# Silu made from Tanh, and products taken out of PSUM in their own step, in the first stage of a two-layer kernel

## The chip, the cores and the metric

The kernel runs on one core of a Trainium2 chip. The metric is the device time of one execution in microseconds; it is the median over several executions. The core has five queues that work in order and side by side: TensorE (PE, with its weight loads shown as PEld), VectorE (DVE), ScalarE (ACT), GpSimd (POOL) and SyncE (SP), which issues most DMAs.

## The reference

All tensors are fp32. The input x is 8 batches of 512 tokens of 256 channels. The first layer adds a state-space branch and an FP4-quantized gated network to x; the second layer adds two attention branches. Only the first layer is touched:

```
xn   = layernorm(x)
# branch 1: selective scan, 512 inner channels, 16 states
xin, z = split(xn @ W_in.T)
u    = silu(conv4(xin) + conv_b)              # causal, per channel
dt, B, C = split(u @ W_xproj.T)
delta = softplus(dt @ W_dt.T + b_dt)
h_t  = exp(delta_t * A) * h_{t-1} + (delta_t * u_t) * B_t
y    = (sum_n h * C + D * u) * silu(z)
out1 = y @ W_out.T
# branch 2: weights, xn and h are rounded to blocks of 16 FP4 values with a scale
h    = silu(fp4(xn) @ fp4(w_gate).T) * (fp4(xn) @ fp4(w_up).T)
out2 = fp4(h) @ fp4(w_down).T
x    = x + out1 + out2
```

## The kernel before

The work of the first layer, called the first stage, is written as one program order for all engines: in this stage every engine executes its instructions exactly in the order in which the Python program issues them, and every instruction has the helper's line, L53, in the profile. Its instructions are therefore told apart by the names of their tiles.

**The scan loop.** The backbone is a loop over g, 256 steps: 8 batches, 4 channel chunks of 128, and 8 pairs of the 16 states. Step g issues, in this order: the load of C for step g + 2 (tile cb, on SP's queue); `scan`, two VectorE scans of 128x512 (hh from da and bu); `decay` for step g + 2, two ScalarE Exp (da); in odd steps `inputs`, 16 small groups of PE matmuls that spread delta*u times B over the states into the one PSUM buffer bu, which serves the next two steps and so can't begin before the odd step's scans have ended; `sum_states`, PE transposes that add the states of earlier steps into y; one `step()` of the strands; and `times_c`, GpSimd's product of hh with C.

**The strands.** All other work is cut into generators, called strands, which advance by one stage in each `step()`, by rank. `z` and `finish` come first (the gate z of a chunk, and y's way out through a transpose to the product with z), then `output` (W_out), then the delta strands and `diagonals`, then `head` (layer norm, transposes xt, projections, convolution, u, and the product ps_xp), then `ffn` (branch 2), then the FP4 rounding of the weights. `head` of batch b + 1 starts 16 steps before batch b does; while the next but one step of the loop has not its delta, du and B ready (`able`), `step()` is called again without a scan, so that the loop stands still.

A strand's stages are given as functions to `skewed`, which runs one stage of each unit per step. A stage that makes a product on PE allocates one of three PSUM banks (MM = 3, tag mm); the tuple at a stage says how many banks it frees and takes, and a strand is passed over in a step if it would take more than are free. In the kernel before, a product and its way out of PSUM are two stages, so a bank is held from one step into the next. The ones that matter:

- `head`: `project` (PE, ps_in), `tap0` (ScalarE, cv = first tap and bias), `taps12` and `tap3` (VectorE, three multiply-adds that read ps_in and cv), `silu` (ScalarE, u): five steps, two between the starts of two chunks. Then ps_xp, and in the next step its copies xd and xb.
- The delta strand: `rank` (PE, ps_dt), `parts` (ScalarE: Relu, Abs, Exp, Copy), `rests` (VectorE, tile e), `logs` (ScalarE, Ln), `deltas` (GpSimd, from the second batch on), `turned` (PE, ps_du), `put_du` (ScalarE): seven steps; a chunk every three steps.
- `ffn`, for each of 4 token tiles: the gate's product (ps_gu from w_g); a step later ScalarE's Silu into h and the up product (ps_gu from w_u); a step later VectorE's h * ps_gu; this for two halves of 352 columns, then the FP4 rounding (q_m on ScalarE, q_l and q_v on VectorE, q_v and h on GpSimd), the transposes `to_inner` (ps_i, taken out into ht) and w_down (ps_d).
- `z`: the product ps_z; a step later ScalarE's Silu into z.
- `finish`: ScalarE's copy of y (into the tile delta), PE's transpose ps_y, VectorE's u * D + ps_y, GpSimd's product with z.

ScalarE holds one function table at a time; where the next function isn't in it, the program has an ACT_TABLE_LOAD ahead of that instruction. The functions of this stage are Exp, Ln, Sqrt, Silu, and Identity, Copy, Abs and Relu, ahead of which no load stands.

The second layer's stage follows, with other loops and no Silu; it is not part of the change.

Of the kernel before, what the change touches and what calls it, by code (L numbers as in the profile page):

```python
# [9 lines left out]
FP = mybir.dt.float32  # L10
BF = mybir.dt.bfloat16
AF = mybir.ActivationFunctionType
ALU = mybir.AluOpType
# [4 lines left out]
P = 128  # L18
# [40 lines left out]
def tile_kernel(ctx: ExitStack, tc: tile.TileContext, a: dict, out: bass.AP):  # L59
# [57 lines left out]
    with ExitStack() as s0:  # L117
# [36 lines left out]
        def constants():  # L154
            act.activation(a_neg, a_neg, AF.Exp)
            dve.tensor_scalar(a_neg, a_neg, -1.0, None, ALU.mult)
            dve.tensor_reduce(four, ident.rearrange("p (r n) -> p n r", n=QL), AX.X, ALU.add)
            n = FI - (NI - 1) * P
            for t in (w_d, *hts):
                pool.memset(t[n:, NI - 1, :], 0.0)  # L160

        w_g = w0.tile([P, KC, FI], FP, name="w_g")
        w_u = w0.tile([P, KC, FI], FP, name="w_u")
        def skewed(units, stages, every):


            made = {}
            stages = [s if isinstance(s, tuple) else (s, 0, 0) for s in stages]
            for step in range((len(units) - 1) * every + len(stages)):
                todo = [(i, stages[step - i * every]) for i in range(len(units)) if 0 <= step - i * every < len(stages)]  # L170
                peak = held = 0
                for _, (_, frees, takes) in todo:
                    held += takes - frees
                    peak = max(peak, held)
                yield peak, held
                for i, (f, _, _) in todo:
                    made[i] = f(units[i], made.get(i))
# [86 lines left out]
        def to_inner(dst, then=()):  # L264


            def turn(src, c0, c1):
                ps = pmm.tile([P, L], FP, tag="mm", name="ps_i")
                for c in range(c0, c1):
                    n = min(P, FI - c * P)  # L270
                    pe.transpose(ps[:n, (c - c0) * P : (c - c0 + 1) * P], src[:, c * P : c * P + n], ident)
                return src, ps

            def both(unit, st):
                src, ps = st
                out = dst(unit)
                act.copy(out[:, :4, :], ps.rearrange("p (c n) -> p c n", n=P))
                return out, turn(src, 4, NI)[1]

            def last(unit, st):  # L280
                out, ps = st
                n = FI - (NI - 1) * P
                act.copy(out[:, 4, :], ps[:, :P])
                act.copy(out[:n, 5, :], ps[:n, P : 2 * P])
                return out

            return [(lambda _, src: turn(src, 0, 4), 0, 1), (both, 1, 1), (last, 1, 0)]

        def fp4_weights():
# [14 lines left out]
            def turn(unit, raw):  # L304
                ps = pmm.tile([P, L], FP, tag="mm", name="ps_w")
                for k in range(KC):
                    for i in range(2):
# [4 lines left out]
                        )  # L312
                return ps

            def put(unit, ps):
                name, at = unit
                dst = w_g if name == "w_gate" else w_u
                act.copy(
                    dst[:, :, at * FB : (at + 2) * FB],
                    ps[:, : 4 * FB].rearrange("p (k n) -> p k n", k=KC),  # L320
                )

            down = to_inner(lambda unit: w_d[:, :, unit[1] * P : (unit[1] + 1) * P])
            units = [(name, j) for j in range(0, FI // FB, 2) for name in ("w_gate", "w_up")]
            stages = [fetch, idle, *fp4_stages(FB, 2 * D), (turn, 0, 1), (put, 1, 0)]
            yield from skewed(units, stages, 2)
# [31 lines left out]
        def head(b):  # L358
# [29 lines left out]
            def turn(k, _):  # L388
                ps = pmm.tile([P, L], FP, tag="mm", name="ps_tr")
                for t in range(NT):  # L390
                    pe.transpose(ps[:, t * P : (t + 1) * P], xn[:, t, k * P : (k + 1) * P], ident)
                return ps

            def put(k, ps):
                act.copy(xt[:, k, :], ps)

            yield from skewed(range(KC), [(turn, 0, 1), (put, 1, 0)], 1)

# [4 lines left out]
            def project(c, _):  # L403
                ps = pmm.tile([P, L], FP, tag="mm", name="ps_in")
                for k in range(KC):
                    pe.matmul(
                        ps, w_in[:, k, c * P : (c + 1) * P], xt[:, k, :], start=(k == 0), stop=(k == KC - 1)
                    )
                return ps

# [4 lines left out]

            def tap0(c, ps):
                cv = rot.tile([P, L], FP, tag="cv", bufs=2, name="cv")
                act.activation(
                    cv, ps, AF.Identity, scale=conv_w[:, c, 3:4], bias=conv_b[:, c : c + 1]
                )  # L420
                return ps, cv

            def taps12(c, st):
                tap(st[1], st[0], c, 1)
                tap(st[1], st[0], c, 2)
                return st

            def tap3(c, st):
                ps, cv = st
                tap(cv, ps, c, 3)  # L430
                return cv

            def silu(c, cv):
                u_.setdefault(b, []).append(w1.tile([P, L], FP, tag="u", bufs=2 * NC + 2, name="u"))
                act.activation(u_[b][c], cv, AF.Silu)

            while b - 3 in u_:
                yield 0, 0
            stages = [(project, 0, 1), tap0, taps12, (tap3, 1, 0), silu]
            yield from skewed(range(NC - 2), stages, 2)  # L440
# [4 lines left out]
            while b > 1 and (b - 2, NC - 1) not in ready:  # L445
                yield 0, 0
            yield 1, 1
            ps = pmm.tile([P, L], FP, tag="mm", name="ps_xp")
            for c in range(NC):
                pe.matmul(ps, w_xp[:, c, :], u[c], start=(c == 0), stop=(c == NC - 1))  # L450
            yield 0, -1
            xd = w1.tile([P, L], FP, tag="xd", bufs=1, name="xd")
            act.copy(xd, ps)
            xb = rot.tile([P, L], FP, tag="e", bufs=3, name="xb")[:NS]
            act.copy(xb.rearrange("n (t r j) -> n r t j", t=NT, j=QL), ps[:NS].rearrange("n (r t j) -> n r t j", t=NT, j=QL))
            c_d = dram.tile([NS, L], FP, tag="c_d", name="c_d")
            sp.dma_start(c_d, xd[RC : RC + NS, :])
            diags = diags_[b] = []

            def diagonals():  # L460
# [10 lines left out]
                for i in range(NS // 4):  # L471
                    yield (0, -1) if i == NS // 4 - 1 else (0, 0)
                    bd = rot.tile(shape, FP, tag="bd", bufs=2 * (NS // 4) - 1, name="bd")
# [8 lines left out]
            def rank(c):  # L482
                ps = pmm.tile([P, L], FP, tag="mm", name="ps_dt")
                pe.matmul(ps, w_dt[:, c * P : (c + 1) * P], xd, start=True, stop=True)
                return ps

            def parts(c, ps):
# [5 lines left out]
                act.activation(w, ps, AF.Copy, bias=1.0)  # L493
                return ps

# [18 lines left out]
            def turned(c, _):  # L514
                ps = pmm.tile([P, L], FP, tag="mm", name="ps_du")
                for t in range(NT):
                    pe.transpose(ps[:, t * P : (t + 1) * P], du[b, c][:, t * P : (t + 1) * P], ident)
                return ps

            def put_du(c, ps):  # L520
                act.copy(du[b, c], ps)
                ready.add((b, c))

            by = pool if b else dve
            begin(diagonals(), 2)
            stages = [
                (lambda c, _: rank(c), 0, 1), parts, (rests, 1, 0), logs, deltas, (turned, 0, 1), (put_du, 1, 0),
            ]
# [8 lines left out]
        def ffn(b):  # L537
# [14 lines left out]
            def turn_x(k, _):  # L552
                ps = pmm.tile([P, L], FP, tag="mm", name="ps_tr")
                for t in range(NT):
                    pe.transpose(ps[:, t * P : (t + 1) * P], xn[:, t, k * P : (k + 1) * P], ident)
                return ps

            def put_x(k, ps):
                act.copy(xqt[:, k, :], ps)

            yield from skewed(range(KC), [(turn_x, 0, 1), (put_x, 1, 0)], 1)
            quantized.add(b)
# [11 lines left out]
            def gate_up(half):  # L574
                cols = slice(half * n, (half + 1) * n)

                def gate(t, h):
                    return h, product(t, w_g, cols)

                def up(t, st):  # L580
                    h, ps = st
                    act.activation(h[:, cols], ps[:, :n], AF.Silu)
                    if half and t == NT - 1:
# [19 lines left out]

            def begin(t, _):
                return gate0(t, q.tile([P, FI], FP, tag="q_src", bufs=4, name="h"))

            (gate0, up0, both0), (gate1, up1, both1) = gate_up(0), gate_up(1)
            stages = [
                (begin, 0, 1), (up0, 1, 1), (lambda t, st: gate1(t, both0(t, st)), 1, 1), (up1, 1, 1), (both1, 1, 0),
                *fp4_stages(P, FI),  # L610
# [113 lines left out]
        def z(b, c):  # L724
            yield 1, 1
            ps = pmm.tile([P, L], FP, tag="mm", name="ps_z")
            for k in range(KC):
                pe.matmul(
                    ps, w_in[:, k, DI + c * P : DI + (c + 1) * P], made[b][1][:, k, :],
                    start=(k == 0), stop=(k == KC - 1),  # L730
                )
            yield 0, -1
            t = z_[b, c] = rot.tile([P, L], FP, tag="z", bufs=2, name="z")
            act.activation(t, ps, AF.Silu)
            through.add((b, c))

        def finish(b, c):


            rows = delta.pop((b, c))  # L740
            act.copy(rows, ys.pop((b, c)))
            yield 1, 1
# [38 lines left out]
        def step():  # L781
            for s, (peak, kept) in list(active.items()):
                if held[0] + peak <= MM:
                    held[0] += kept
                    active[s] = next(s, None)
                    if active[s] is None:
                        del active[s]

        begin(head(0), 3)
# [722 lines left out]
```

## Time and profile before

| | us |
|---|---|
| time, median of 3 runs | 3333.97 (3328.56 to 3334.05) |
| the profiled execution: its own time | 3343.63 |
| the profiled execution: span from first to last instruction | 3341.5 |
| first scan of the first stage starts | 47.9 |
| PE busy over the span | 2983.8 |
| DVE busy | 2191.1 |
| ACT busy | 1811.5 |
| POOL busy | 1534.9 |
| all ACT_TABLE_LOADs of the first stage (266 of 1283 ns) | 341.3 |

In the profile's lines an entry such as `cv<-ps_in` names the tile written and the tiles read; "xN" counts instructions; behind a bar stand busy time in us, mean ns of one, and the engine's idle time just before them with what ended it. A wait "DVE e <- ACT du" says that VectorE's instruction that writes e waited for ScalarE's that writes du. The windows view gives the busy us of each engine in stretches of the span. The chain of waits follows the work that ended last back to what released it.

### The profile page before, as it was taken

How to read it: one execution, taken by the hardware profiler on the slowest of the kernel's cores; microseconds unless marked ns; L12 is line 12 of the kernel's file. 1: busy time of each engine (PE TensorE's matmuls, PEld its weight loads, DVE VectorE, ACT ScalarE, POOL GpSimd, SP SyncE). 2: the span in 40 equal slices, each digit the busy share in tenths (PEclk: the TensorE clock that was granted, in tenths of full speed). 3: DMA queues.
4: the chain of work that ended last, by engine and by line, in shares of the span. 5: the costliest groups of instructions: out<-in, count | busy, mean ns of one | idle time of the engine just before them, and what ended most of it. 6: DMA issues, size and time to landing. Idle time of an engine off the chain costs nothing.

```text
span 3341.5 us, 50483 instructions
## 1 busy us (share of the span) xinstructions
PE 2983.8 (89%) x19012; PEld 1820.8 (54%) x19012; DVE 2191.1 (66%) x4298; ACT 1811.5 (54%) x3588; POOL 1534.9 (46%) x1100
## 2 busy tenths in 40 slices
PE   5567888788888887999999999999999999999998
PEld 3445665656666666546545545545545545545545
DVE  5769787878777876656557556556556546556554
ACT  7576878687887875334334434434433533533533
POOL 2776777787878796213213322312312412412412
PEclk7778999899999999899999999999999999999999
DMA  3323333334333433210110110110110110110110
GB/s 117 114 90 121 118 120 115 108 127 133 108 127 116 131 120 108 97 34 33 65 34 32 65 34 32 65 34 32 65 34 32 65 34 32 65 34 32 59 34 7
DMA packets 93802, 244.42 MB, mean 73 GB/s; under 512 B 9848, under 2 KB 46712, under 8 KB 93560
## 3 DMA queue, kind: packets, MB, share of 16 engines
q1 hardware_dynamic: 92408, 237.01, 21.5%
q10 hardware_dynamic: 1152, 4.19, 0.3%
q8 instruction: 151, 2.47, 0.3%
q14 instruction: 91, 0.75, 0.1%
HBM read 231.48 MB, written 9.70 MB: 72 GB/s over the span
## 4 chain that ended last, share of the span: by engine, by line
PE 64%; DVE 20%; ACT 9%; issue 3%; POOL 2%; DMA 1%; DVEq 0%; ACTq 0%; POOLq 0%; SPq 0%
PE ps_qkv L1165 10%; DVE hh L53 9%; PE ps_g L1344 5%; PE ps_a L1344 4%; PE bu L53 4%; PE ps_wo L1308 3%; PE y L53 3%; PE lo L1278 3%; ACT L53 3%; PE ps_y L1379 3%; PE ps_w L1362 3%; PE ps_gu L53 2%; PE pt L1264 2%; PE ps_ls L1217 2%; PE pt_qk L1156 2%
## 5 line engine op out<-in xcount | busy, mean ns | idle before, releaser
L53 POOL TENSOR_TENSOR hh<-hh,cb 128x1024 f32<-128x1024 f32 x256 | 607.2, 2378 | 244.0 <-DVE hh L53 158.7
L53 DVE TENSOR_TENSOR_SCAN hh<-da,bu 128x512 f32<-128x512 f32 x512 | 591.8, 1200 | 94.2 <-PE bu L53 85.0
L53 ACT ACTIVATE da<-delta,a_neg 128x512 f32<-128x512 f32 x512 | 341.1, 715 | 38.7 <-DVE hh L53 36.7
L53 ACT ACT_TABLE_LOAD x266 | 341.3, 1283 | 20.6 <-DVE ln_mv L53 7.1
L53 PE MATMUL bu<-bd,du 32*128 32x128 f32 x4096 | 174.2, 314 | 164.3 <-DVE hh L53 155.6
L1255 POOL TENSOR_TENSOR pr<-pr,lrs 128x512 f32<-128x512 f32 (+1 forms) x256 | 234.6, 933 | 179.3 <-DVE lrs L1253 141.4
L53 PE MATMUL y<-ident,hh 128*128 128x128 f32 x2048 | 304.6, 299 | 6.5 <-ACT delta L53 3.7
L1184 POOL TENSOR_TENSOR r<-r,r 128x512 f32<-128x512 f32 x128 | 162.8, 1272 | 287.7 <-DVE r L1182 242.3
L1236 ACT ACTIVATE pr<-ps_ls,nm 128x256 f32<-128x256 f32 (+1 forms) x512 | 221.5, 448 | 125.2 <-DVE nm L1230 122.7
L53 PEld LDWEIGHTS y<-ident,hh 128*128 128x128 f32 x2048 | 257.6, 154 | 56.3 <-issue 27.1
L53 PEld LDWEIGHTS bu<-bd,du 32*128 32x128 f32 x4096 | 148.5, 214 | 224.0 <-issue 148.8
L1350 ACT ACTIVATE gl<-ps_g,b 128x512 f32<-128x512 f32 x96 | 65.9, 686 | 306.2 <-PE ps_g L1344 306.2
L1082 ACT ACTIVATE pt_e<-ps_st 128x512 f32<-128x512 f32 x320 | 166.7, 597 | 108.0 <-PE ps_st L1076 101.8
L1180 DVE TENSOR_TENSOR r<-ps_qkv,tab 128x512 f32<-128x512 f32 x128 | 88.2, 689 | 201.0 <-ACT sq L1179 195.1
L920 POOL MEMSET sa<- 128x1 f32 x16 | 1.6, 98 | 451.8 <-DVE sf L1366 358.6
L1125 POOL TENSOR_TENSOR x1s<-x1s,bsum 128x256 f32<-128x256 f32 x32 | 23.2, 724 | 373.8 <-DVE x1s L1124 373.8
L1230 DVE CUSTOM_DVE_ANT_0 ps_ls<-ps_ls,mask 128x256 f32<-128x256 f32 (+1 forms) x512 | 184.3, 422 | 7.4 <-PE ps_ls L1217 6.7
L1344 PE MATMUL ps_g<-hn,wf 128*128 128x512 f32 x384 | 184.5, 603 | 4.0 <-DVE hn L1333 2.6
L1165 PE MATMUL ps_qkv<-wqkv,sf 128*128 128x512 f32 x384 | 182.4, 608 | 0.0
L1165 PE MATMUL ps_qkv<-wqkv,s 128*128 128x512 f32 x384 | 181.3, 608 | 0.3 <-DVE r L1182 0.3
L1351 DVE SCALAR_TENSOR_TENSOR ht<-ps_a,b,gl 128x512 f32<-128x512 f32 x80 | 60.0, 750 | 157.8 <-PE ps_a L1344 155.1
L1264 PE MATMUL pt<-ident,pr 128*128 128x128 f32 x896 | 132.9, 284 | 33.2 <-POOL pr L1255 28.2
(219 smaller groups left out, 6308.9 us busy)
## 6 DMA issues: line engine op xcount, KB each, us to landing
cb<-c_d SPq DMA_DIRECT2D x256, 512.0 KB, 3.7
wqkv<-in_wqkv SPq DMA_DIRECT2D x16, 1536.0 KB, 7.8
wf<-in_wf SPq DMA_DIRECT2D x16, 1408.0 KB, 6.1
wf<-in_wf SPq DMA_DIRECT2D x16, 768.0 KB, 9.2
tab<-tab SPq DMA_DIRECT2D x16, 512.0 KB
wo<-in_wo SPq DMA_DIRECT2D x16, 512.0 KB, 3.8
xl<-in_x SPq DMA_DIRECT2D x8, 512.0 KB, 4.0
x<-in_x SPq DMA_DIRECT2D x8, 512.0 KB, 5.9
```

What stands on the lines that cost most here:

```text
L53: return self.tc.keep_in_program_order(getattr(self.engine, name)(*args, **kwargs))
L1082: act.activation(pt, banks[g], AF.Exp)
L1165: pe.matmul(ps, shifted(s, k, t * P, P), wqkv[:, k, i * IN : (i + 1) * IN], start=(k == 0), stop=(k == KC - 1),)
L1184: pool.tensor_tensor(r1[:, i], r1[:, i], r2, ALU.add)
L1230: last = dve.tensor_tensor_reduce(at, at, msk[:, 2 * P - nk :], -1.0, 3e38, ALU.add, ALU.min, nm[:, i : i + 1])
L1236: act.activation(pr[:, at], banks[r][:, at], AF.Exp, bias=nm[:, i : i + 1], scale=-1.0, accum_out=rs[:, i : i + 1],)
L1255: pool.tensor_tensor(ph, ph, rs.unsqueeze(2).to_broadcast([P, 2, nk]), ALU.mult)
L1264: pe.transpose(pt[:, j * P : (j + 1) * P], pr[:, j * P : (j + 1) * P], ident)
L1278: pe.matmul(o[r * LD : (r + 1) * LD, i * P : (i + 1) * P], lv[:, keys[j], h * LD : (h + 1) * LD], prts[r][:, (i * nkt + j) * P : (i * nkt ...
L1308: pe.matmul(ps, wo[:, c, m * P : (m + 1) * P], ot[:, c, :], start=(c == 0), stop=(c == IN // P - 1),)
L1344: pe.matmul(dst, wf1[:, k, off : off + P], hn[:, k, :], start=(k == 0), stop=(k == KC - 1))
L1362: pe.matmul(ps, wf2[:n, c, m * P : (m + 1) * P], ht[c][:n], start=(c == 0), stop=(c == NHC - 1),)
```

## The change

Four things are done together, all in the first stage.

1. Silu is made of Tanh: silu(x) = (tanh(x/2) + 1) * x/2. The halves are put into weights: GpSimd multiplies conv_w, conv_b and the z half of w_in by 0.5 at the start, and the copy of w_gate's rounded, transposed weights out of PSUM has a scale of 0.5. ScalarE computes Tanh; a VectorE operation then does (t + 1) * x. For u both of its tensors lie in SBUF (u and cv); for z and the gate the second lies in PSUM (ps_z, ps_gu).
2. ScalarE's work that takes a product out of PSUM is no longer a stage of its own in the next step. `behind` puts it on a list, `late`, which `step()` issues behind all strands' other work of the same step. So strands become shorter: the convolution has four steps in place of five, the delta strand five in place of seven, `to_inner` two in place of three, and the transposes, ps_xp, ps_du and ps_w one less each. `finish`'s copy of y goes behind as well.
3. The bank counts have a fourth number, `briefly`: a bank that is taken and taken out in the same step counts within the step, and is given back at its end.
4. The three taps are one stage, and `diagonals` issues two of its four products in a step in place of one.

The diff, cut to its core:

```diff
 def constants():
+            for t in (conv_w, conv_b, w_in[:, :, DI:]):
+                pool.tensor_scalar(t, t, 0.5, None, ALU.mult)
...
+        late = []
+        def behind(f):
+            late.append(f)
 def skewed(units, stages, every):
-                for _, (_, frees, takes) in todo:
-                    held += takes - frees
+                for _, (_, frees, takes, briefly) in todo:
+                    held += takes + briefly - frees
                     peak = max(peak, held)
-                yield peak, held
+                    brief += briefly
+                yield peak, held, brief
...
-            return [(lambda _, src: turn(src, 0, 4), 0, 1), (both, 1, 1), (last, 1, 0)]
+            return [(first, 0, 0, 1), (last, 0, 0, 1)]
...
-                act.copy(
+                act.activation(
                     dst[:, :, at * FB : (at + 2) * FB],
                     ps[:, : 4 * FB].rearrange("p (k n) -> p k n", k=KC),
+                    AF.Copy, scale=0.5 if name == "w_gate" else 1.0,
                 )
...
 def project(c, _):
-                return ps
+                cv = rot.tile([P, L], FP, tag="cv", bufs=2, name="cv")
+                behind(lambda: act.activation(
+                    cv, ps, AF.Identity, scale=conv_w[:, c, 3:4], bias=conv_b[:, c : c + 1]
+                ))
+                return ps, cv
-            def tap0(c, ps):
-            def taps12(c, st):
-            def tap3(c, st):
+            def taps(c, st):
                 ps, cv = st
-                tap(cv, ps, c, 3)
+                for k in range(1, 4):
+                    tap(cv, ps, c, k)
                 return cv
+            def tanh(c, cv):
+                u_.setdefault(b, []).append(w1.tile([P, L], FP, tag="u", bufs=2 * NC + 2, name="u"))
+                act.activation(u_[b][c], cv, AF.Tanh)
+                return cv
             def silu(c, cv):
-                act.activation(u_[b][c], cv, AF.Silu)
+                dve.scalar_tensor_tensor(u_[b][c], u_[b][c], 1.0, cv, ALU.add, ALU.mult)
-            stages = [(project, 0, 1), tap0, taps12, (tap3, 1, 0), silu]
+            stages = [(project, 0, 1), (taps, 1, 0), tanh, silu]
...
-            yield 1, 1
+            yield 1, 1, 1
             ps = pmm.tile([P, L], FP, tag="mm", name="ps_xp")
-            yield 0, -1
+            def split():
                 act.copy(xd, ps)
                 act.copy(xb..., ps...)
                 sp.dma_start(c_d, xd[RC : RC + NS, :])
+            behind(split)
+            yield 0, 0
...
 def rank(c):
                 pe.matmul(ps, w_dt[:, c * P : (c + 1) * P], xd, start=True, stop=True)
+                behind(lambda: parts(c, ps))
                 return ps
 def turned(c, _):
+                def put():
+                    act.copy(du[b, c], ps)
+                    ready.add((b, c))
+                behind(put)
-                (lambda c, _: rank(c), 0, 1), parts, (rests, 1, 0), logs, deltas, (turned, 0, 1), (put_du, 1, 0),
+                (lambda c, _: rank(c), 0, 1), (rests, 1, 0), logs, deltas, (turned, 0, 0, 1),
...
 def gate(t, h):
-                    return h, product(t, w_g, cols)
+                    ps = product(t, w_g, cols)
+                    behind(lambda: act.activation(h[:, cols], ps[:, :n], AF.Tanh))
+                    return h, ps
 def up(t, st):
-                    act.activation(h[:, cols], ps[:, :n], AF.Silu)
+                    dve.scalar_tensor_tensor(h[:, cols], h[:, cols], 1.0, ps[:, :n], ALU.add, ALU.mult)
                     return h, product(t, w_u, cols)
...
 def z(b, c):
+            t = rot.tile([P, L], FP, tag="z", bufs=2, name="z")
+            behind(lambda: act.activation(t, ps, AF.Tanh))
             yield 0, -1
-            act.activation(t, ps, AF.Silu)
+            dve.scalar_tensor_tensor(t, t, 1.0, ps, ALU.add, ALU.mult)
 def finish(b, c):
-            act.copy(rows, ys.pop((b, c)))
+            y = ys.pop((b, c))
+            behind(lambda: act.copy(rows, y))
             yield 1, 1
...
 def step():
+            brief = 0
-            for s, (peak, kept) in list(active.items()):
+            for s, (peak, kept, *briefly) in list(active.items()):
                 if held[0] + peak <= MM:
                     held[0] += kept
+                    brief += sum(briefly)
                     active[s] = next(s, None)
+            for f in late:
+                f()
+            late.clear()
+            held[0] -= brief
```

## The prediction

> **What bounds the kernel now.** First the windows view, cut where the first and the last scan stand: before the scans, the scan loop, two places where one scan waits long for the next, one undisturbed batch, and all that follows.
>
> ```profile
> core 0: us, PE busy (x) PEld busy (x) DVE busy (x) ACT busy (x) POOL busy (x), PEclk, DMA share, GB/s
> 0.00:47.90 47.90, 24.96 (x82) 11.23 (x82) 17.64 (x33) 27.70 (x39) 1.38 (x10) 0.82 0.44 128
> 47.90:1305.70 1257.80, 994.27 (x8164) 745.34 (x8165) 997.00 (x1146) 969.37 (x1370) 974.49 (x564) 0.90 0.36 118
> 538.40:554.00 15.60, 10.15 (x79) 7.31 (x78) 7.40 (x13) 12.19 (x18) 9.70 (x6) 0.88 0.30 101
> 850.80:869.10 18.30, 12.21 (x84) 7.66 (x82) 8.40 (x13) 16.94 (x25) 15.82 (x11) 0.96 0.24 87
> 1023.50:1167.70 144.20, 122.20 (x1035) 90.70 (x1034) 118.38 (x130) 109.12 (x155) 112.99 (x64) 0.94 0.39 128
> ...
> 1341.50:3341.50 2000.00, 1937.59 (x10639) 1043.19 (x10637) 1162.56 (x3089) 805.90 (x2165) 544.47 (x508) 0.99 0.13 44
> ```
>
> The change touches the first stage only, so the last 2000 us stay. In the loop of 1257.8 us (256 steps, 4.9 us each) the four engines are busy 994, 997, 969 and 974 us: each about 78%, none the bound. What a step costs is the waiting of in-order queues for each other. Now the chain of waits, in the loop's window:
>
> ```profile
> by line: DVE hh L53 22.7%; PE bu L53 9.9%; PE y L53 8.2%; ACT L53 7.0%; PE ps_gu L53 6.3%; issue 4.8%; ACT da L53 4.2%; PE ps_d L53 3.5%; DVE q_v L53 3.0%; PE ps_xp L53 2.0%; DVE cv L53 2.0%; PE ps_o L53 2.0%; DVE q_l L53 1.9%; ACT du L53 1
> ```
>
> "ACT L53" without a tile is the table load: 7.0% of 1257.8, 88 us. DVE's shares shown add to 29.6%. Next, ScalarE's queue in order of time around one Silu:
>
> ```profile
> 310.75 1.28 ACT L53 ACT_TABLE_LOAD   x1
> 312.04 0.46 ACT L53 ACTIVATE h<-ps_gu 128x352 f32<-128x352 f32 x1
> 312.40 0.62 ACT L53 ACTIVATE q_m<-q_v 128x512 bf16<-128x512 f32 x1
> 313.04 1.28 ACT L53 ACT_TABLE_LOAD   x1
> 314.33 1.33 ACT L53 ACTIVATE da<-delta,a_neg 128x512 f32<-128x512 f32 x2
> ```
>
> One load into Silu, one back to the Exp of the decays. Then VectorE's groups by form in the loop (busy us, mean ns, idle before and its releasers):
>
> ```profile
> L53 DVE TENSOR_TENSOR h<-h,ps_gu 128x352 f32<-128x352 f32 x62 | 32.0, 516 | 80.6 <-PE ps_gu L53 74.7 <-ACT h L53 4.0 <-ACT da L53 1.7
> L53 DVE SCALAR_TENSOR_TENSOR q_v<-q_v,q_l 128x512 f32<-128x512 f32 x16 | 29.6, 1848 | 2.1 <-DVE q_l L53 0.5
> ...
> L53 DVE SCALAR_TENSOR_TENSOR u<-u,d_par,ps_y 128x512 f32<-128x512 f32 x31 | 22.5, 727 | 5.8 <-PE ps_y L53 5.6
> ```
>
> The q_v operation reads two SBUF tensors; from the tile's view, the spread of all its forms (min/median/max ns):
>
> ```profile
> L53 DVE SCALAR_TENSOR_TENSOR q_v<-q_v,q_l x58: 686/1748/2837, 91.1 to 1318.6; 128x704 f32<-128x704 f32 x34, 128x512 f32<-128x512 f32 x16, 88x512 f32<-88x512 f32 x8
> ```
>
> Last, waits in the loop (us, times, longest): VectorE's three longest in sum, then ScalarE's longest.
>
> ```profile
> DVE hh L53 <- PE bu L53: 85.0, 64, 4.0
> DVE h L53 <- PE ps_gu L53: 74.7, 35, 6.2
> DVE e L53 <- ACT du L53: 40.2, 17, 7.9
> ```
>
> ```profile
> ACT delta L53 <- PE y L53: 124.4, 30, 9.9
> ```
>
> And in VectorE's order of time, the rests (e) at two of the turns from a batch to the next:
>
> ```profile
> 214.62 0.69 DVE L53 SCALAR_TENSOR_TENSOR e<-du,ps_dt 128x512 f32<-128x512 f32 x1 [7.88 <-ACT du L53]
> ...
> 551.88 0.69 DVE L53 SCALAR_TENSOR_TENSOR e<-du,ps_dt 128x512 f32<-128x512 f32 x1 [6.71 <-ACT du L53]
> ```
>
> **A. Table loads go.** Walking ScalarE's instructions of the first stage in order, 266 loads stand there: 46 ahead of a gate's Silu, 31 of a z's, 23 of a u's (several Silus run on one load), 32 ahead of a Ln, 8 of a Sqrt, and 126 back to Exp. If Tanh needs no table other than Exp's, there remain 32 + 8 and 40 ways back: 80. So 186 x 1.283 = 239 us leave ScalarE, whose loop falls from 969 to about 730 us. What of it was on the path: 88 us x 186/266 = 62 at most. The least I take from 850.8:869.1, where POOL is busy 15.82 beside ScalarE's 16.94, so that 7% is gained before the next engine holds: some 10 allowing for hand-overs. In the whole loop PE and DVE stand level with ScalarE, so I take the half: 31 us gained (10 to 62). That Tanh shares Exp's table no row shows. [...]
>
> **B. VectorE multiplies.** 28 u, 32 z and 63 gates in the loop. z reads one PSUM and one SBUF tensor like the u<-u,d_par,ps_y row: 32 x 0.727 = 23 us. Gates like h<-h,ps_gu: 63 x 0.516 = 33. The u multiplication reads two SBUF tensors like q_v: 28 x 1.848 = 52 (at 0.686 to 2.837: 19 to 79). I take the mean row, because POOL is as busy then as now. Together 108 us (75 to 135); DVE goes from 997 to 1105, which in the present loop would be 88%, while no engine passes 85% in the undisturbed batch (PE 122.2 of 144.2). On the path: at least the chain's 29.6%, 32 us; at most all, 108; I take half, 54, because some land in odd steps, where VectorE waits for bu anyway (85.0 us in 64 waits). [...]
>
> **C. One step less between product and VectorE.** Before, the taps and rests ran two steps behind PE; z and the gates went to ScalarE alone. Now taps, rests, z and gates all stand in VectorE's in-order queue one step behind the product, with ScalarE's part between; behind each the next scan is queued, and behind that the bu matmuls (one buffer) and POOL's product. The row for a product taken in the next step is h<-ps_gu: 35 of 62 wait. ScalarE's part newly in the way: 63 x 0.463 (gates) + 28 x 0.772 (cv) + 32 x 0.598 (z) = 70 us, x 35/62 = 39. Rests wait 40.2 already with a step more; behind the rank product stand four activations (2.5 us), which now come sooner in ScalarE's queue: I keep 40, bounds -40 to +75. Some of these waits coincide within a step or replace the one for bu: I take 25 (0 to 115). ScalarE also waits at a step's end; what is queued behind is the decay of two steps ahead, whose lead covers it: nothing, or, without that cover, the next scan waits as for PE.
>
> **D. Shorter strands.** From xp to the first ready du there are four steps less (conv one, xp one, rank's strand two), and a bank taken out in its own step blocks fewer strands. At three batch turns a scan starts 22.4 (198.6 to 221.0), 15.6 and 18.3 us (two steps) after the one before, because the new batch's delta is not ready: 56.3 - 4 x 4.9 = 37 us over. The work there stays; the busiest engine, ScalarE, worked 14.2, 12.2 and 16.9 us of these, which leaves 13. I take 15 gained (0 to 37).
>
> **E. The y copy moves behind.** ScalarE waits 124.4 us for y at the head of its step with the strands' work behind; at the end it blocks less. ScalarE is then no bound: 5 gained (0 to 10). The c_d write leaves one step earlier, past the cb loads on SP's queue, which lead by two steps: nothing. Paired bd products: same work.
>
> **F. Start and end.** Before the first scan two loads go (2.6 us); a last u multiplication (0.7) and GpSimd's halving of conv_w, conv_b and half of w_in come, POOL being busy 1.4 of 47.9 us; if PE's projection waits for the latter, some 2.4 us (the 128x1024 product's time). Zero (-3 to +4). The scale of 0.5 in w_g's copies is free (same instruction).
>
> **Sum.** -31 + 54 + 25 - 15 - 5 + 0 = +28 us. The profiled execution took 3343.6 us (span 3341.5), 9.6 above the median of 3334.0; made against itself it becomes 3372, which against the median is 3362.
>
> **Rivals.** *ScalarE was the hidden bound (faster).* Place: the batch turns, where rests wait 7.88 and 6.71 us for ScalarE, and the steps in which decays come behind loads. Price: A 62, D 25, E 5 against B 45 and C 10: -37, 3297. It decides once A and D together pass B + C = 79 less E, so with D at 15 only when nearly all 62 us of loads count. For it: the 7.0%. Against: PE and DVE level with ScalarE. *VectorE becomes the bound:* all of B, C at 60, less 31, 15 and 5: +116, 3450. For it: 88%; against: its 85 us of bu waits can be filled. *The loads stay* (Tanh in another set than Exp): A is nothing, +59, 3393. *No change:* terms cancel, within 6.7 us (0.2%, about what a measurement here can tell).
>
> **How the numbers follow.** Forecast (7 to 75 us slower) 0.47; VectorE bound 0.13; loads stay 0.04; no change 0.07; ScalarE bound 0.29. So slower 0.64, same 0.07, faster 0.29. All terms good give -75, all bad over +200, not together; from -48 to +92, 3286 to 3426, a tenth is left out at each end. The likeliest case's own range is 3341 to 3409.
>
> **What would show it.** Right: some 80 loads in the first stage; ACT near 730 us in the loop; DVE near 1105; u<-u,cv near 1.8 us; new DVE waits for ACT h, z and cv; no scan gap above 15 us; the loop 20 to 45 us longer. Wrong: DVE above 90% of a shorter loop, or its waits for PE and ACT below the present 200 us in sum; that would mean that banks and ScalarE had held the strands.

## The result

The changed kernel takes 3362.5 us (median; 3361.4 to 3364.0) against 3334.0 before: ratio 1.0088, interval 1.0070 to 1.0105. The forecast, slower by 28 us, is met almost exactly; the experiments show that it is a difference of larger terms, of which several were mis-sized.

Its profiled execution took 3363.3 us, span 3361.3. First the windows view of the changed kernel, with the columns of the prediction's: before the scans, the scan loop, the batch from 1050.7, and the last 2000 us.

```profile
0.00:49.70 49.70, 25.85 (x80) 11.38 (x80) 20.66 (x38) 23.31 (x36) 4.57 (x13) 0.79 0.39 123
49.70:1335.40 1285.70, 1003.48 (x8170) 767.93 (x8171) 1066.51 (x1269) 724.29 (x1186) 980.63 (x563) 0.89 0.34 115
...
1050.70:1204.40 153.70, 123.98 (x1045) 94.13 (x1044) 128.28 (x148) 87.97 (x144) 120.93 (x69) 0.94 0.36 118
1361.30:3361.30 2000.00, 1933.68 (x10648) 1039.66 (x10648) 1165.88 (x3102) 809.44 (x2168) 545.79 (x509) 0.99 0.13 44
```

The loop is 28 us longer (1285.7 for 1257.8). ScalarE fell to 724 us, VectorE rose to 1067, now the busiest. VectorE's busy time in the loop grew by 70 us and its idle time fell by 42, from 261 to 219 us; the difference is the 28 us. The chain of waits in the loop agrees on ScalarE: the table load ("ACT L53") has 1.1% where it had 7.0%.

```profile
by line: DVE hh L53 16.6%; PE bu L53 8.0%; PE y L53 7.8%; PE ps_gu L53 4.8%; issue 4.5%; PE ps_d L53 3.2%; DVE q_v L53 2.8%; DVE cv L53 2.5%; PE ps_z L53 1.9%; PE ps_in L53 1.7%; PE ps_xp L53 1.3%; PE ps_o L53 1.2%; ACT L53 1.1%; DVE q_l L5
```

VectorE's groups by form in the loop. First the first tap in the kernel before; then, in the changed kernel, the three new multiplications, and the taps and rests, which now wait for ScalarE.

```profile
L53 DVE SCALAR_TENSOR_TENSOR cv<-ps_in,conv_w,cv 128x511 f32<-128x511 f32 x28 | 20.4, 727 | 0.0
```

```profile
L53 DVE SCALAR_TENSOR_TENSOR u<-u,cv 128x512 f32<-128x512 f32 x28 | 32.5, 1162 | 0.0
L53 DVE SCALAR_TENSOR_TENSOR h<-h,ps_gu 128x352 f32<-128x352 f32 x63 | 32.2, 512 | 47.6 <-ACT h L53 47.5
...
L53 DVE SCALAR_TENSOR_TENSOR z<-z,ps_z 128x512 f32<-128x512 f32 x31 | 20.9, 675 | 9.9 <-ACT z L53 9.7
L53 DVE SCALAR_TENSOR_TENSOR cv<-ps_in,conv_w,cv 128x511 f32<-128x511 f32 x28 | 20.8, 744 | 25.5 <-ACT cv L53 25.4
L53 DVE SCALAR_TENSOR_TENSOR e<-du,ps_dt 128x512 f32<-128x512 f32 x30 | 20.5, 684 | 31.4 <-ACT du L53 31.2
```

The new work is 32.5 + 32.2 + 20.9 = 86 us. That VectorE's busy time grew by 70 alone is mainly due to q_v's operations of 128x704, which fell from 65.3 to 51.0 us; no run was made to learn why. The first tap, which never waited before (0.0), now waits 25.4 us for ScalarE. No gap between scans is left like the 22.4 and 15.6 us at the batches' turns before; the widest is 11.8 us. But the batch from 1050.7 takes 153.7 us, where the undisturbed one of before took 144.2.

### The profile page after: what moved, and what is told of

Its sections match the earlier page's. It is cut to its first block, busy times and chain, and to the rows that moved or that the text cites. A ratio compares the mean times of both kernels' runs of the same rounds, so it can differ in the third digit from the quotient of the medians.

```text
span 3361.3 us, 50387 instructions
## 1 busy us (share of the span) xinstructions
PE 2984.9 (89%) x19012; PEld 1836.9 (55%) x19012; DVE 2263.7 (67%) x4426; ACT 1562.5 (46%) x3399; POOL 1545.1 (46%) x1103
## 4 chain that ended last, share of the span: by engine, by line
PE 62%; DVE 17%; ACT 4%; issue 3%; POOL 2%; DMA 1%; DVEq 0%; POOLq 0%; ACTq 0%; SPq 0%
PE ps_qkv L1190 10%; DVE hh L53 6%; PE ps_g L1369 5%; PE ps_a L1369 4%; PE ps_wo L1333 3%; PE bu L53 3%; PE y L53 3%; PE lo L1303 3%; PE ps_y L1404 3%; PE ps_w L1387 3%; PE pt L1289 3%; PE ps_ls L1242 2%; PE ps_gu L53 2%; PE ps_st L1103 2%; DVE nm L1056 2%
## 5 line engine op out<-in xcount | busy, mean ns | idle before, releaser
L53 POOL TENSOR_TENSOR hh<-hh,cb 128x1024 f32<-128x1024 f32 x256 | 612.6, 2401 | 263.7 <-DVE hh L53 147.8
L53 DVE TENSOR_TENSOR_SCAN hh<-da,bu 128x512 f32<-128x512 f32 x512 | 592.3, 1199 | 65.3 <-PE bu L53 62.9
L53 PE MATMUL bu<-bd,du 32*128 32x128 f32 x4096 | 185.4, 328 | 253.7 <-DVE hh L53 240.5
L53 ACT ACTIVATE da<-delta,a_neg 128x512 f32<-128x512 f32 x512 | 338.4, 715 | 19.4 <-DVE hh L53 17.3
L53 PEld LDWEIGHTS bu<-bd,du 32*128 32x128 f32 x4096 | 158.3, 226 | 310.4 <-issue 207.5
L53 PE MATMUL y<-ident,hh 128*128 128x128 f32 x2048 | 315.9, 306 | 7.0 <-ACT delta L53 6.4
L53 PEld LDWEIGHTS y<-ident,hh 128*128 128x128 f32 x2048 | 266.5, 158 | 55.7 <-issue 27.3
L1369 PE MATMUL ps_a<-hn,wf 128*128 128x512 f32 x320 | 150.4, 592 | 0.0
```

Of the source, the lines that this page charges most:

```text
L53: return self.tc.keep_in_program_order(getattr(self.engine, name)(*args, **kwargs))
L1369: pe.matmul(dst, wf1[:, k, off : off + P], hn[:, k, :], start=(k == 0), stop=(k == KC - 1))
```

## The experiments

Theory 1 is the prediction's. Theory 2: the loads were hidden. Theory 3: ScalarE did hold the kernel before, and the new order spoils the gain. All intervals are of the ratio to the kernel before, which was run again beside every experiment, with medians from 3334.0 to 3336.0 us: a difference between medians from different experiments is known no better than those 2 us.

**Table loads alone.** In the kernel before:

```diff
-act.activation(u_[b][c], cv, AF.Silu)      (and the gate's and z's)
+act.activation(u_[b][c], cv, AF.Tanh)
```

> The kernel before with Tanh in place of Silu at its three places and nothing else (the halves and the multiplication are left out, so that the function is another one): the table loads alone. Theory 1 (the prediction's: ScalarE's loads were worth a part of their path share, VectorE's work and waits cost more): 186 loads fewer, 31 us faster, 3303 (3272 to 3324). Theory 2 (the loads were hidden; all of the loss is something else): 3325 to 3334. Theory 3 (ScalarE held the kernel before, the new order spoils it): 3270 or less.

Measured 3297.5 us, 0.9881 (0.9868 to 0.9893): 38.5 us faster. The windows view of its loop, from 48.0 to 1266.0:

```profile
48.00:1266.00 1218.00, 977.62 (x8160) 737.63 (x8161) 998.91 (x1146) 726.20 (x1185) 975.20 (x563) 0.91 0.36 122
```

243 us left ScalarE and the loop lost 40: one in six. Tanh needs no load beside Exp: 80 loads are left of 266, and in the trace of the changed kernel ScalarE goes from Exp to Tanh or back 196 times without one. Theory 2 falls.

**The new order alone.** The changed kernel with Silu on ScalarE:

```diff
-behind(lambda: act.activation(h[:, cols], ps[:, :n], AF.Tanh))   (and z's; u as a stage)
+behind(lambda: act.activation(h[:, cols], ps[:, :n], AF.Silu))
-dve.scalar_tensor_tensor(...)               (u, z, gate), halves of the weights
```

> The changed kernel's strands, bank counts and order, but with Silu on ScalarE and no multiplication on VectorE: the new order alone. Theory 1: 20 us gained by shorter strands and by y's copy, 10 lost in the waits of taps and rests: 3324 (3310 to 3335). Theory 3 (the new order is what costs): 3345 or more, with VectorE's waits on ScalarE as in the changed kernel.

Measured 3402.0 us, 1.0196 (1.0182 to 1.0209): 66 us slower, against theory 1, and as theory 3 expected. VectorE's waits in its loop (us, times, longest):

```profile
DVE e L53 <- ACT du L53: 88.3, 26, 9.2
...
DVE cv L53 <- ACT cv L53: 42.6, 23, 3.2
```

The rests (e) wait 88.3 us where they waited 40.2, the taps 42.6 where they waited nothing: one step behind the product, ScalarE's table loads stand between (without them, in the changed kernel, 31.2 and 25.4).

**The multiplications.** The changed kernel without them; the empty stage of u stays:

```diff
-dve.scalar_tensor_tensor(u_[b][c], u_[b][c], 1.0, cv, ALU.add, ALU.mult)   (and z, gate)
```

> The changed kernel without VectorE's 128 multiplications (left out, so the function is another one): VectorE's added work and the waits of z and of the gates go together. Theory 1: the 86 us of added work measured in the loop, half of it on the path, and 15 us of waits: 3362 - 43 - 15 = 3304 (3285 to 3320). Theory 3: 3345 or more. If VectorE is the bound: 3362 - 86 - 57 = 3219.

Measured 3324.8 us, 0.9959 (0.9946 to 0.9973): they cost 37.8 us of 86 us of work, where theory 1 expected 58. Even without them the new order is 27 us behind the one-line edit of the first experiment (3297.5).

**The loads in the new order.** The changed kernel with AF.Silu at its three AF.Tanh:

> The changed kernel with Silu in place of Tanh, the multiplications kept (so the function is another one): its order with the table loads back. Theory 1: ScalarE again near 960 us in the loop, 31 us more: 3393 (3375 to 3425). Theory 2 (loads are hidden): 3362 to 3368.

Measured 3423.8 us, 1.0255 (1.0239 to 1.0271): the loads cost 61 us here, and 77 in the new order without multiplications (3402.0 - 3324.8), but 38.5 in the old order. It fits that ScalarE's work weighs more where its results are wanted a step earlier.

**Work or wait.** The multiplications on 8 columns:

```diff
-dve.scalar_tensor_tensor(t, t, 1.0, ps, ALU.add, ALU.mult)
+dve.scalar_tensor_tensor(t[:, :8], t[:, :8], 1.0, ps[:, :8], ALU.add, ALU.mult)   (u, gate alike)
```

> The changed kernel with the 128 multiplications narrowed to 8 columns (the rest of u, z and the gates keeps tanh alone): each still waits for ScalarE, but does next to no work. It splits the 38 us that the multiplications cost together. Theory 1 (work on the path counts about half of its 86 us, waits the rest): 3325 + 5 to 15 = 3330 to 3340. Rival (the wait for ScalarE is the whole price): 3355 to 3362. Rival (work is the whole price): 3325.

Measured 3329.6 us, 0.9981 (0.9972 to 0.9989). The narrow operations still take 26 us in the loop (9.7 the gates', 11.7 u's, 4.6 z's), so that 60 of the 86 us of work are gone, and 33 us of time with them: about half. The other 5 of the 37.8 us are all that is left for those 26 us and for the waits. The gates wait 49.8 us for ScalarE in this kernel too and z's multiplications 11.9, but VectorE's idle time in the loop is 250 us here and 254 in the kernel without multiplications: these waits stand in place of others. The h multiplication, which waited 74.7 us for PE before, now waits 10.6.

```profile
DVE h L53 <- ACT h L53: 49.8, 26, 3.7
...
DVE h L53 <- PE ps_gu L53: 10.6, 15, 2.6
```

**One step less.** An idle stage puts the taps and the rests two steps behind their products again:

```diff
-stages = [(project, 0, 1), (taps, 1, 0), tanh, silu]
+stages = [(project, 0, 1), lambda _, x: x, (taps, 1, 0), tanh, silu]
-(lambda c, _: rank(c), 0, 1), (rests, 1, 0), logs, ...
+(lambda c, _: rank(c), 0, 1), lambda _, x: x, (rests, 1, 0), logs, ...
```

> The changed kernel with an idle step between the product and VectorE's part for the taps and the rests, as far behind as before. If the one step less is what the new order costs (waits for ScalarE's cv 25 us and e 31 us go, half of it on the path): 20 to 28 us less, 3335 to 3343. If the order costs by something else (bank counts, more strands in a step, y's copy): 3355 to 3370.

Measured 3310.0 us, 0.9925 (0.9907 to 0.9943; its executions lie between 3300.7 and 3321.6): 52.6 us, give or take 6, less than the changed kernel, twice what was expected, and faster than the one before. The windows view of its loop, and the groups, which show the two waits gone (0.0 and 2.2 us idle ahead):

```profile
50.50:1289.30 1238.80, 986.21 (x8170) 744.00 (x8171) 1049.77 (x1269) 724.79 (x1189) 981.56 (x563) 0.90 0.36 120
```

```profile
L53 DVE SCALAR_TENSOR_TENSOR cv<-ps_in,conv_w,cv 128x511 f32<-128x511 f32 x28 | 20.6, 734 | 0.0
L53 DVE SCALAR_TENSOR_TENSOR e<-du,ps_dt 128x512 f32<-128x512 f32 x30 | 19.9, 664 | 2.2 <-ACT du L53 2.1
```

25.5 + 31.4 - 2.2 = 55 us of VectorE's waits went and 52.6 us of time. That the two sums agree doesn't show that they are the same microseconds, since other waits moved:

```profile
DVE z L53 <- ACT z L53: 31.2, 12, 4.5
DVE x L53 <- PE ps_d L53: 29.5, 18, 2.9
```

These were 9.7 and 14.5 us in the changed kernel; the gates' wait for ScalarE fell, from 47.5 to 25.5. In all, VectorE's idle time in the loop fell by 30 us, from 219 to 189, and its busy time by 17: q_v's operations (all shapes) took 77 us in place of 96, u's 4.6 us more. So a part of the gain, 17 of the 47 us between the two profiled loops, is not a wait at all.

**Taps alone.** The idle stage ahead of the taps only:

> The changed kernel with the idle step ahead of the taps alone; the rests stay one step behind their product. It splits the 52 us of the idle steps. If both count by VectorE's waits in the changed kernel (25 for cv, 31 for e): about 23 of 52, 3339. If the delta strands' rests are what counts, because they stand at the batches' turns: 3355 to 3363. If the taps are nearly all: 3310 to 3320.

Measured 3340.6 us, 1.0021 (1.0013 to 1.0030): 21.9 of the 52.6 us, close to the ratio of the two waits, as expected; the rests have the other 30.7. By the profiled loops VectorE's idle time falls by 25 us with the taps' step, to 194, as much as the taps had waited. The rests' step takes away 5 us more of idle time, although the rests had waited 42.4 us there, and 13 us of busy time.

**The old strands.** The kernel before with Tanh, halves and multiplications, where only the gates' and z's Tanh go behind:

```diff
-stages = [(project, 0, 1), tap0, taps12, (tap3, 1, 0), silu]
+stages = [(project, 0, 1), tap0, taps12, (tap3, 1, 0), tanh, silu]
```

> The kernel before with Tanh, the halves and the multiplications alone: copies out of PSUM stay a stage of their own, only the Tanhs of gates and z are issued behind the step. By the terms measured so far, 3297 for the loads and 38 for the multiplications: 3335 (3325 to 3345), level with the kernel before. If the strands and bank counts of the change are needed to make room for the multiplications: 3350 or more.

Measured 3406.9 us, 1.0220 (1.0207 to 1.0233): 109 us above the kernel with Tanh alone, not 38. VectorE's scans on both sides of a batch's turn of this kernel:

```profile
543.43 2.32 DVE L53 TENSOR_TENSOR_SCAN hh<-da,bu 128x512 f32<-128x512 f32 x2
...
575.26 2.32 DVE L53 TENSOR_TENSOR_SCAN hh<-da,bu 128x512 f32<-128x512 f32 x2
```

31.8 us lie between the two; 29.4, 22.4 and 15.6 at other turns, 13.5 elsewhere. The five are 112.7 us where steps of 4.9 would be 24.5: 88 us over. In the kernel with Tanh alone the five longest (22.5, 15.6, 10.3, 10.1 and 9.6) are 44 over, so that some 44 of the 109 us are longer stands of the loop, at the turns above all, where the strands that make delta come too late. The changed kernel has no such stands: its longest is 11.8 us. Where the rest of the 109 us lies isn't shown; VectorE's busy time in the loop is 87 us above that of the kernel with Tanh alone (1086 for 999), its idle time 24 us (243 for 219). This kernel's convolution also has a step more than the one before, six for five, and no run tells that step from the multiplications.

**The bank counts.** The changed kernel, with a brief bank counted to the end of the next step:

```diff
-held[0] -= brief
+held[0] -= owed[0]
+owed[0] = brief
```

> The changed kernel with its brief banks counted to the end of the next step, so that fewer strands pass in a step. If the freer count crowds the steps and that is what the new order costs: 3335 to 3350. If the count helps (strands come earlier, no step without a scan): 3368 to 3390. If neither: 3358 to 3367.

Measured 3423.9 us, 1.0265 (1.0252 to 1.0278): 61 us more. The freer count is worth that much against this stricter one, which is not the old one exactly.

**One step more for others.** From the version with both idle steps, one more ahead of z's multiplication and of the addition of ps_d; then of the latter alone:

```diff
+yield 0, 0                                      (z, ahead of its yield 0, -1)
-(down, 0, 1), (add, 1, 0),
+(down, 0, 1), lambda _, x: x, (add, 1, 0),
```

> The kernel with both idle steps, and one more idle step ahead of z's multiplication and of the addition of ps_d, where VectorE still waits 31 and 30 us. If a wait of VectorE costs where it stands, at half of it as before: 30 us less, 3280. If these strands then hold banks so long that others are passed over: 3310 to 3335.

> The kernel with both idle steps and one more ahead of the addition of ps_d alone, z as it was. It takes the 25 us lost with both apart. If z's later step was the loss: 3295 to 3310. If the bank that ps_d holds a step longer was: 3325 to 3340.

Measured 3335.0 (0.9998; 0.9985 to 1.0010) and 3332.3 us (0.9991; 0.9982 to 1.0000): 25 and 22 us worse than with the two idle steps, although VectorE's 29.5 us of waits for ps_d went. So the loss is the later addition's. That the bank it holds a step longer is the reason isn't shown. In the profiled loops of the version with both idle steps and of the one with the later addition, VectorE is idle for 189 us each; the second is 14 us longer because VectorE is busy longer, 1064 for 1050, and q_v's operations take 91 us in place of 77. In the kernel before, the 4 of 128x704 that start while GpSimd is idle take 0.89 us, the 28 that start while it works 2.20 in the mean, so that another order in time may change their sum. That is a rival to the bank, and no run separates them.

**u on GpSimd.** From the version with both idle steps:

```diff
-dve.scalar_tensor_tensor(u_[b][c], u_[b][c], 1.0, cv, ALU.add, ALU.mult)
+act.activation(u_[b][c], u_[b][c], AF.Copy, bias=1.0)
+pool.tensor_tensor(u_[b][c], u_[b][c], cv, ALU.mult)
```

> The kernel with both idle steps, u's multiplication moved: ScalarE adds 1 to the tanh (0.6 us, it has room), GpSimd multiplies by cv (1.27 us like its other 128x512 products). VectorE loses 32 operations of 1.16 us, 33 us in the loop; at the share that the multiplications showed (33 us for 86 us of work) 13 us less: 3297. If GpSimd's queue carries it to the scans (980 us busy becomes 1016, and its products with C come later): 3310 to 3330.

Measured 3292.0 us, 0.9867 (0.9853 to 0.9880), the fastest kernel here with the whole function, 42.7 us under the one before. Its loop in the windows view:

```profile
48.40:1260.90 1212.50, 968.14 (x8170) 731.39 (x8171) 1024.25 (x1241) 738.87 (x1217) 1011.37 (x591) 0.92 0.37 122
```

By the medians this is 18 us less than with both idle steps, where 13 were expected. By the profiled executions, of which the one with both idle steps was 7 us above its median, the loop is 26 us shorter (1212.5 for 1238.8): VectorE gave up 26 us of work, its idle time is 188 us as before, and GpSimd took 30.

## Why the prediction was right, and where it was not

The measured steps add up along this path: 3336.0 before (its median beside these runs), -38.5 for the loads (Tanh alone), +27.3 for the new order without multiplications, +37.8 for the multiplications: but for rounding the 3362.5. In the prediction's terms the three are A, then C with D and E, then B, for which it had -31, +5 and +54. So A was too small by 8, C with D and E too small by 22, and B too large by 16. The size of the sum, 27 us for 28, is luck in part: the errors cancel. One by one:

- **A, loads, -31.** Right in size: -38.5 in the old order, within 10 to 62. 186 loads fewer were counted; 189 went. That Tanh would need no load beside Exp, which no row of before showed, held.
- **B, multiplications, +54.** Over: 37.8 us in the new order. The step that failed is the price of u: q_v's mean of 1.848 us was taken, measured is 1.162, with a median of 0.668 and a maximum of 2.967. At least half of them are as fast as z's, which have one input in PSUM (0.675). So the work was 86 us and not 108. The half that was taken as the share on the path held: 33 us of time for 60 us of work. In the changed kernel's loop the 13 u multiplications that start while GpSimd is idle take 0.660 to 0.668 us, the 15 that start while it works 1.59 in the mean and up to 2.967; z's take 0.68 and 0.67 in the two cases.
- **C, one step less, +25.** Half of what two idle steps take off the changed kernel, 52.6 us, for taps and rests alone. The waits on ScalarE that it forecast are there (57 us in the trace after), but how much of the 52.6 is these waits stays open, since VectorE's idle time fell by 30 us and its busy time by 17. For z and the gates it was right that waits replace others: together with 26 us of narrow operations they cost 5 us.
- **D and E, shorter strands, banks, y's copy, -20.** Measured only together with C. Without multiplications the three cost 27.3 us; if the idle steps would save 52.6 there too, which no run shows, D and E gain some 25, an estimate that is near the 20. Behind the multiplications they are worth more: the change takes 44.4 us off the kernel that has the multiplications in the old strands. The prediction read the price from the gaps of the kernel before (37 us over) and did not ask how these grow when a stage is added. E was not tried alone.
- **F, start, 0.** The first scan comes 1.7 us later; within its bounds. With the scale w_g's four copies take 0.454 us each, where they took 0.441: near to free, as it had them.

Of the signs that it named for being right, VectorE near 1105 us (1067) and u near 1.8 us did not come, the others did. A sign of being wrong came as well: VectorE's three longest waits, 200 us in sum before, are 142 after (62.9 for bu, 47.5 for the gates' Tanh, 31.2 for the rests). What it stood for, ScalarE and banks that held the kernel, was half true: the loads' 38.5 us were there to be had, and the versions with idle steps have them. The rival of VectorE as the bound appears in no run: it is busy for 83% of the changed kernel's loop, and for 82% of the loop with the old strands.

## What to carry to other kernels

Between in-order queues, count for each consumer how many steps it stands behind its producer, and what its own queue holds behind it: a step of distance at two places was worth 53 us here, more than the 38 us that 243 us less work on another engine gave, while other waits of the same engine cost next to nothing because they stood in place of others. Take a stage out of a strand for its bank or its latency, but try to keep the distance with an idle stage, place by place: at the taps and rests it gained, ahead of ps_d's addition it lost 22 us. And test a bundle of edits by its parts: edits that seemed to need each other held a loss of 53 us that two idle stages take away. Look at an engine's busy time as well as at its waits: q_v's operations took from 77 to 106 us in these loops, with the same work.

## What the runs showed of the hardware

The same PE instructions of the loop, some 8170 matmuls, took 968 us of busy time in the fastest loop, at a mean granted clock of 0.92, 978 at 0.91 with Tanh alone, and 1003 at 0.89 in the changed kernel. Busy time times clock is 890 to 893 us in all three, so the longer time goes with the lower clock. The mean is made of two values: in the kernel before, the windows view cut to 3.2 us shows the full clock in one window and half of it in the next.

```profile
62.20:65.40 3.20, 1.31 (x28) 0.81 (x29) 3.17 (x5) 3.17 (x5) 2.27 (x2) 1.00 0.23 79
65.60:68.80 3.20, 3.20 (x22) 2.98 (x18) 3.17 (x3) 3.12 (x7) 1.67 (x1) 0.50 0.31 116
```

Every clock record of that trace is 1.0 or 0.5 (59 of each), and all but the last are 3.41 us long or a multiple of it. Cut to that length, the loop has 74 stretches at half clock and 295 at full clock. PE was busy for 34% (median) of the 3.41 us ahead of one at half clock, and for all (median) of the 3.41 us ahead of one at full clock; in the trace of the changed kernel it was 33% and all. So in these two traces the lower clock follows a PE that waited. Part of each difference between these kernels may then feed itself; no run holds the clock fixed, so neither this nor its size is shown.
